# Output products of all four batches as seven for eight, and softmax totals by one transfer inside SBUF

## The chip, the cores and the metric

The kernel runs on one core of a Trainium2 chip. The core has a matmul engine (TensorE, PE in the profile), a vector engine (VectorE, DVE), an activation engine (ScalarE, ACT), a general engine (GpSimd, POOL) and a sync engine (SyncE, SP), which in this kernel issues every DMA. Each engine works through its own instructions in order and waits on semaphores. The on-chip memories are SBUF (128 partitions) and PSUM, where matmuls put their sums. The metric is the device time of one execution in microseconds (us); a run of the kernel is compared with others by the median.

## The reference

Everything is float32: 4 batches (B), 1024 tokens (N), width 1024 (DIM), 16 heads of 64.

```python
scale, shift = split(cond @ W_emb + b_emb)              # per batch
xn  = rms_norm(x, g_norm) * (1 + scale) + shift
q, k, v = split_heads(xn @ W_qkv)                       # (1024 x 1024) @ (1024 x 3072) per batch
q, k = rms_norm(q, g_q), rms_norm(k, g_k)
o   = softmax(q @ k.T / 8) @ v                          # per batch and head
x   = x + o + o @ W_out                                 # (1024 x 1024) @ (1024 x 1024) per batch
x   = x + causal_conv(x, taps = cond) + conv_bias       # 4 taps per channel; the taps are the 4 rows of cond
```

The part that this change is about is `x + o + o @ W_out` and the convolution behind it, and, in the softmax, the division by the sum of the exponentials.

## The kernel before

**Units.** Attention is cut into 64 units: for every batch b (4) and every pair of heads c (8), two halves of the queries (512 each). Unit p is batch p // 16, pair p // 2 % 8, half p % 2. A unit's scores are 8 key tiles of 128 x 1024 (`scores`, L683: matmul, copy to SBUF on ScalarE, running maximum on VectorE). The softmax (`softmax`, L732) takes the maximum over partitions on GpSimd, copies it to PSUM, subtracts on VectorE (`shift`), exponentiates on ScalarE and adds up on GpSimd (`weigh`). The unit's product with the values (`values`, L746) and its totals (`finish`, L760) are computed while the next unit's scores run. There is one PSUM tile for the product with the values (`ps_a`), so the next unit can begin its own only when `divide` (L799) has read the previous one.

**The totals.** `finish` sums the exponentials over the partitions with a matmul by ones: four groups of 256 totals, in partitions 0, 32, 64 and 96. `spread` (L781) copies them to SBUF, writes the four rows to DRAM in four transfers and reads them back as 128 partitions of 8. `invert` (L791) takes the reciprocal of this small tile on VectorE, writes it to DRAM and reads it back, repeated over the partitions, as `rec`. `divide` multiplies the product by `rec` into `oT` and stores it in DRAM (`scrO`). For the last pair of batch 3 both halves skip this way: their reciprocal is taken on the whole PSUM tile (L804), and `oT` stays in SBUF.

**The other work.** Between the stages of a unit a list of pieces runs on TensorE. Seven pieces a unit belong to x @ W_qkv (`Double.piece`, L638), which is done in Winograd's form of Strassen's scheme, seven block products for eight, for two head pairs at a time. In the units before unit 60 they fill most of the time; the last of them runs in unit 59.

**The output products.** With the block rows of o by token half and the block columns by half of the width, `o @ (W_out + 1)` is 8 products of 4 matmuls (128 x 128 by 128 x 512) for 4 output blocks (two halves of tokens, columns j and j + 4). A `Quad` (L897) computes these 4 blocks with 7 products, P1 to P7, in the order P1, P2, P6, P5, P3, P7, P4. Four of its operands are sums of blocks of o, written to DRAM by `OutSums` (L871), and four are sums of blocks of the weights, written by `OutWeights` (L842). Each product loads 1 MB of o (tag `ob`, two buffers) and 256 KB of weights (tag `wo`, three buffers). Partial sums u2 and u4 stay in SBUF. 70 such products, the ten quads of batches 0 and 1 and j = 0, 1 of batch 2, are laid into units 18 to 59 (`products_until`). The other 8 blocks of batch 2 and the 16 of batch 3 are `Out` blocks (L963): two products each (8 matmuls), whose o is loaded once (`gather`, L817) and held; VectorE adds the identity to the weights (`diagonal`, L987). Batch 2's 8 blocks lie in units 60 to 62. Of batch 3's, seven lie in unit 63 and nine behind it.

**A block's end.** x is transposed into PSUM (`residual`), the products are added, and the result, x1, is put into SBUF: with a ScalarE copy in `Out`, with a VectorE addition of u2 or u4 in `Quad`. ScalarE makes the last tap, VectorE the other three (`taps`, L1042), with a halo of three columns that the first half of the tokens leaves for the second. Later `store` transposes the result on TensorE, copies it on ScalarE and stores it.

**What sets the order.** The instructions of TensorE, VectorE, ScalarE and GpSimd run in the order in which the program emits them. A model clock moves with each emitted TensorE step (`tick`); steps for other engines are put off by so many microseconds of that clock (`defer`), into a gap after the maximum (`defer_gap`), or to the end of the softmax's busy time (`defer_quiet`), and `need` emits what has been put off when someone depends on it. SP's transfers are placed by the framework, as early as their buffers allow in its plan, and run in that order.

Of the kernel before, what the change touches and what calls it, by code (L numbers as in the profile page):

```python
# [15 lines left out]
P = 128  # L16
# [5 lines left out]
def kernel(  # L22
# [148 lines left out]
    rows = apool.tile([P, HN], F32, tag="xs", name="rows", bufs=2)[:NR, :P]  # L171
# [39 lines left out]
    class Norm:  # L211
# [10 lines left out]
        def squares(self, i):  # L222
            t0 = self.tiles[i] * P
            for g in range(2):
                xs = apool.tile([P, HN], F32, tag="xs", name=f"xs_{self.name}_{i}_{g}", bufs=2)
                nc.sync.dma_start(xs, x[self.b, t0 : t0 + P, g * HN : (g + 1) * HN])
                defer(5.0 + g, ("x", self.name), lambda xs=xs, g=g: self.square(xs, xs, i, g))
# [4 lines left out]
        def squares_of(self, i, halves):  # L232
            for g in range(2):
                to = apool.tile([P, HN], F32, tag="xs", name=f"xs_{self.name}_{i}_{g}", bufs=2)
                self.square(halves[g], to, i, g)
# [145 lines left out]
    class Embed:  # L381
# [22 lines left out]
        def run(self):  # L404
# [11 lines left out]
            sb = apool.tile([P, HN], F32, tag="xs", name=f"mod_sb_{half}", bufs=2)[:, :QN]  # L416
# [260 lines left out]
    class Unit:  # L677
        def __init__(self, pr, half):
            self.pr, self.half = pr, half
            self.name = f"{pr.b}_{pr.c}_{half}"  # L680
            self.sp = []

# [77 lines left out]
        def finish(self):  # L760
            b, c = self.pr.b, self.pr.c
            tot = ps_m.tile([P, HN], F32, tag="m", name=f"tot_{self.name}")
            for g in range(4):
                h, i = divmod(g, 2)
                some = slice(0, HN) if (b, c) == (B - 1, NJ - 1) else slice(i * QN, (i + 1) * QN)
# [9 lines left out]
            if (b, c) == (B - 1, NJ - 1):  # L775
                return
            key = ("tot", self.name)
            defer(0.2, key, lambda: self.spread(tot))
            defer(8.0, key, self.invert)

        def spread(self, tot):  # L781
# [3 lines left out]
            scr = dram.tile([4, QN], F32, tag=f"tot_{self.name}", name=f"scrT_{self.name}")  # L785
            for g in range(4):
                nc.sync.dma_start(scr[g : g + 1, :], sums[32 * g : 32 * g + 1, :QN])
            self.few = small.tile([P, 2 * HN // P], F32, tag="few", name=f"few_{self.name}", bufs=1)
            nc.sync.dma_start(self.few, scr.rearrange("g (p i) -> (g p) i", p=32))
# [9 lines left out]
        def divide(self):  # L799
            b, c = self.pr.b, self.pr.c  # L800
            need("tot", self.name)
            if (b, c) == (B - 1, NJ - 1):
# [3 lines left out]
            nc.vector.tensor_mul(oT, self.pav, self.rec)  # L806
            if (b, c) == (B - 1, NJ - 1):
# [9 lines left out]
    def gather(b, half):  # L817

        for kh in range(2):

            n = KH - kh if b == B - 1 else KH
            for k in range(n):
                need("oT", b, kh * KH + k, half)
            if half:
                four = apool.tile([P, 8, QN], F32, tag="r", name=f"ob_{b}_{kh}_{half}", bufs=2)
                four = four.rearrange("p i t -> p (i t)").rearrange("p (k t) -> p k t", t=HN)
            else:
                four = apool.tile([P, KH, HN], F32, tag="ob", name=f"ob_{b}_{kh}_{half}", bufs=2)
            nc.sync.dma_start(four[:, :n, :], scrO[b][half][:, kh * KH : kh * KH + n, :])
            for k in range(n):  # L830
                oTs[b, kh * KH + k, half] = four[:, k, :]
# [64 lines left out]

    class Quad:  # L897


        def __init__(self, b, j):  # L900
            self.b, self.j = b, j
            self.outs = {
# [4 lines left out]
        def load(self, name):  # L907
            b, j = self.b, self.j
            if name in self.outs:
                self.outs[name].load_x()  # L910
            o = self.o[name] = apool.tile([P, KH, HN], F32, tag="ob", name=f"o_{b}_{j}_{name}", bufs=2)
            if name in OUT_S:
                for k in range(KH):
                    need("S", b, k)
                src = scrS[b][:, OUT_S[name], :, :]
            else:
                half, kh = {"P1": (0, 0), "P2": (0, 1), "P4": (1, 1)}[name]
                for k in range(kh * KH, (kh + 1) * KH):
                    need("oT", b, k, half)
                src = scrO[b][half][:, kh * KH : (kh + 1) * KH, :]  # L920
            nc.sync.dma_start(o, src)
# [4 lines left out]

        def product(self, name):
            b, j = self.b, self.j
            out = self.outs.get(name)
            if name == "P7":  # L930
# [3 lines left out]
            if name in ("P2", "P3", "P4"):  # L934
                out.residual()
                pm = out.pm
            else:
                pm = ps_m.tile([P, 512], F32, tag="m", name=f"po_{b}_{j}_{name}")
            for k in range(KH):
                nc.tensor.matmul(  # L940
                    pm,
                    self.w[name][:, k, :],
                    self.o[name][:, k, :],
                    start=(k == 0 and name not in ("P2", "P3", "P4")),
                    stop=(k == KH - 1),
                )
            tick(3.5)
            if name == "P1":
                self.u2 = apool.tile([P, HN], F32, tag="ou2", name=f"ou2_{b}_{j}", bufs=1)
                nc.scalar.copy(self.u2, pm)  # L950
            elif name == "P5":
                self.u4 = apool.tile([P, HN], F32, tag="ou4", name=f"ou4_{b}_{j}", bufs=1)
# [10 lines left out]
    class Out:  # L963
# [12 lines left out]
        def load(self):  # L976
            self.load_x()
            j = self.j
            js = slice(j * P, (j + 1) * P)
            self.w = []  # L980
            for kh in range(2):
                w = wpool.tile([P, KH, P], F32, tag="wo", name=f"wo_{self.name}_{kh}", bufs=3)
                nc.sync.dma_start(w, w_out[kh * HN : (kh + 1) * HN, js].rearrange("(k p) d -> p k d", p=P))
                self.w.append(w)
            defer(4.5, ("wo", self.name), self.diagonal)

        def diagonal(self):  # L987
            d = self.w[self.j // KH][:, self.j % KH, :]
            nc.vector.tensor_tensor(d, d, ident, ALU.add)  # L989

# [13 lines left out]
        def product(self, kh):  # L1004
            b, j, half = self.b, self.j, self.half
            need("wo", self.name)
            need("oT", b, NJ - 1, half)
            for k in range(kh * KH, (kh + 1) * KH):
                nc.tensor.matmul(  # L1009
                    self.pm,  # L1010
                    self.w[kh][:, k % KH, :],
                    oTs[b, k, half],
                    start=False,
                    stop=(k == NJ - 1),
                )
            if kh == 0:
                return
            self.open()
            nc.scalar.copy(self.x1[:, PAD:], self.pm)
            self.last_tap(self.pm)  # L1020

        def open(self):

            if len(taken) == 2:
# [26 lines left out]
        def store(self):  # L1051
# [7 lines left out]
            ot = apool.tile([P, HT, P], F32, tag="x", name=f"ot_{self.name}", bufs=6)  # L1059
# [16 lines left out]
    DIVIDE = 18.0  # L1076
# [5 lines left out]
    LOUD = 5.0  # L1082
    AGE_REST = 5.0
    AGE_OWN = 8.5
    W_AT = 3
# [4 lines left out]
    outs, norms, chunks, weights, doubles, quads = {}, {}, {}, {}, {}, {}  # L1090
    LAST = (B - 1) * 2 * NJ
    NB = 2 * NJ
    ND = B * NJ // 2
    PB = NJ // 2
    LOADS_A = 2

    def piece(T):
# [27 lines left out]
        if n < ND:  # L1125
# [21 lines left out]

            if n in (PB - 1, PB) and i % 14 == W_AT:
                free(lambda: OutWeights((n - PB + 1) * 2 + i // 14).load())
# [19 lines left out]
    def out_next(m):  # L1169
        at = REST.index(m) + 1 if m in REST else 0  # L1170
        out_load(m + 1 if m not in REST else REST[at] if at < len(REST) else LAST)

    def out_load(m):
        if m < B * NB and m not in outs:
            b, i = divmod(m, NB)
# [229 lines left out]
```

## Time and profile before

| | |
|---|---|
| median of 3 runs | 2847.76 us (2844.87 to 2850.12) |
| profiled execution, its own time | 2850.32 us |
| its span, first to last instruction | 2848.5 us |
| TensorE busy | 2764.3 us, 97% of the span |
| VectorE, ScalarE, GpSimd busy | 2162.1, 1541.5, 1323.4 us |
| HBM | 411.85 MB read, 95.40 MB written, 178 GB/s over the span |

The profile has busy time by engine; groups of equal instructions with their count, busy time, mean duration, and the idle time just before them with what ended it; the chain of work that ended last; waits by who waited for whom; and a timeline. A float32 matmul appears as two instructions. Matmuls are pipelined, so the mean duration of one (some 592 ns for 128 x 512) is longer than the distance between two; distances are read from the timeline. Idle time of an engine matters where the engine is on the path that sets the end.

### The profile page before, as it was taken

How to read it: one execution, taken by the hardware profiler on the slowest of the kernel's cores; microseconds unless marked ns; L12 is line 12 of the kernel's file. 1: busy time of each engine (PE TensorE's matmuls, PEld its weight loads, DVE VectorE, ACT ScalarE, POOL GpSimd, SP SyncE). 2: the span in 40 equal slices, each digit the busy share in tenths (PEclk: the TensorE clock that was granted, in tenths of full speed). 3: DMA queues.
4: the chain of work that ended last, by engine and by line, in shares of the span. 5: the costliest groups of instructions: out<-in, count | busy, mean ns of one | idle time of the engine just before them, and what ended most of it. 6: DMA issues, size and time to landing. Idle time of an engine off the chain costs nothing.

```text
span 2848.5 us, 32001 instructions
## 1 busy us (share of the span) xinstructions
PE 2764.3 (97%) x10581; PEld 1315.6 (46%) x10581; DVE 2162.1 (76%) x2579; ACT 1541.5 (54%) x2221; POOL 1323.4 (46%) x534
## 2 busy tenths in 40 slices
PE   6999999999999999999999999999999999999998
PEld 3544444444444445444444445444444444444344
DVE  4578788877888777788777777788778867787863
ACT  4255666655555566655555556565455545555532
POOL 2055554455554454353555355354455445544520
PEclk9999999999999999999999999999999999999999
DMA  9854555645554556674565556665565444533334
GB/s 318 276 170 145 192 174 187 204 152 172 174 196 158 175 192 209 208 234 161 165 208 180 169 180 212 193 228 182 166 214 197 144 135 165 167 104 105 114 108 118
DMA packets 416844, 509.40 MB, mean 179 GB/s; under 512 B 40816, under 2 KB 326824, under 8 KB 406952
## 3 DMA queue, kind: packets, MB, share of 16 engines
q1 hardware_dynamic: 416680, 507.36, 54.6%
q8 instruction: 85, 1.39, 0.2%
q14 instruction: 79, 0.65, 0.1%
HBM read 411.85 MB, written 95.40 MB: 178 GB/s over the span
## 4 chain that ended last, share of the span: by engine, by line
PE 79%; DVE 11%; DMA 4%; ACT 2%; issue 2%; SPq 1%; POOL 0%; DVEq 0%; ACTq 0%; POOLq 0%
PE pqkv_P L648 31%; PE pav L751 16%; PE s L688 15%; PE po L1009 5%; PE po_P L940 5%; DVE mx L705 4%; PE po L940 4%; DVE sp L724 2%; PE qkt L506 1%; DVE qk L498 1%; DMA rec<-scrR 1%; ACT sp L696 1%; PE po L995 1%; PE tot L766 1%; DMA we<-in_L_cond_W_emb_dram 1%
## 5 line engine op out<-in xcount | busy, mean ns | idle before, releaser
L648 PE MATMUL pqkv_P<-w_P,a 128*128 128x384 f32 x3456 | 1177.5, 492 | 18.2 <-issue 6.6
L730 POOL TENSOR_TENSOR sum<-sum,sp 128x1024 f32<-128x1024 f32 x384 | 934.7, 2434 | 35.9 <-ACT sp L728 4.8
L648 PEld LDWEIGHTS pqkv_P<-w_P,a 128*128 128x128 f32 x3456 | 642.4, 191 | 482.7 <-issue 77.7
L696 ACT COPY sp<-s 128x1024 f32<-128x1024 f32 x512 | 501.2, 1017 | 500.1 <-PE s L688 500.0
L728 ACT ACTIVATE sp<-sp 128x1024 f32<-128x1024 f32 x512 | 531.9, 1055 | 221.3 <-DVE sp L724 217.6
L724 DVE TENSOR_TENSOR sp<-sp,mbp 128x1024 f32<-128x1024 f32 x512 | 603.5, 1209 | 21.4 <-ACT mbp L719 21.2
L710 POOL PARTITION_ALL_REDUCE mb<-mx x64 | 219.7, 3432 | 849.7 <-DVE mx L705 421.3
L705 DVE TENSOR_TENSOR mx<-mx,sp 128x1024 f32<-128x1024 f32 x384 | 486.3, 1266 | 133.2 <-ACT sp L696 103.6
L688 PE MATMUL s<-qT,kT 64*128 64x512 f32 x2048 | 509.0, 615 | 2.0 <-ACT sp L696 2.0
L751 PE MATMUL pav<-sp,v 128*64 128x512 f32 x2048 | 484.5, 605 | 17.4 <-DVE oT L806 17.1
L730 POOL TENSOR_TENSOR sum<-sp,sp 128x1024 f32<-128x1024 f32 x64 | 151.5, 2366 | 486.7 <-ACT sp L728 186.5
L688 PEld LDWEIGHTS s<-qT,kT 64*128 64x128 f32 x2048 | 175.6, 185 | 306.3 <-issue 137.6
L751 PEld LDWEIGHTS pav<-sp,v 128*64 128x64 f32 x2048 | 131.6, 137 | 334.5 <-issue 287.4
L1045 DVE SCALAR_TENSOR_TENSOR y<-x,cols,y 128x512 f32<-128x512 f32 x192 | 241.7, 1263 | 48.0 <-ACT y L1033 43.4
L705 DVE TENSOR_TENSOR mx<-sp,sp 128x1024 f32<-128x1024 f32 x64 | 105.2, 1644 | 138.2 <-ACT sp L696 138.2
L667 DVE TENSOR_TENSOR qk<-u,pqkv_P 128x256 f32<-128x256 f32 x256 | 105.7, 413 | 74.0 <-PE pqkv_P L648 73.2
L1009 PE MATMUL po<-ob,wo 128*128 128x512 f32 x352 | 155.4, 593 | 0.5 <-DVE wo L989 0.5
L940 PE MATMUL po_P<-o_P,wq_P 128*128 128x512 f32 x320 | 143.9, 592 | 0.8 <-DMA o_P<-scrS 0.8
L498 DVE TENSOR_TENSOR qk<-qk,ms 128x1024 f32<-128x1024 f32 x64 | 136.0, 2145 | 0.0
L719 ACT COPY mbp<-mb 128x1024 f32<-128x1024 f32 x64 | 65.1, 1017 | 105.6 <-POOL mb L710 105.3
L940 PE MATMUL po<-o_P,wq_P 128*128 128x512 f32 x240 | 108.0, 592 | 0.0
L485 ACT ACTIVATE sq<-qk 128x512 f32<-128x512 f32 x128 | 76.8, 628 | 55.1 <-DVE qk L667 55.1
(94 smaller groups left out, 1753.0 us busy)
## 6 DMA issues: line engine op xcount, KB each, us to landing
a<-scrA SPq DMA_DIRECT2D x212, 512.0 KB
w_P<-scrB SPq DMA_DIRECT2D x64, 768.0 KB
o_P<-scrS SPq DMA_DIRECT2D x40, 1024.0 KB
w_P<-in_L_cond_W_qkv_dram SPq DMA_DIRECT2D x192, 192.0 KB
o_P<-scrO SPq DMA_DIRECT2D x30, 1024.0 KB
scrA<-r SPq DMA_DIRECT2D x28, 896.0 KB
wq_P<-scrW SPq DMA_DIRECT2D x70, 256.0 KB
xc<-in_x_dram SPq DMA_DIRECT2D x64, 256.0 KB
```

What stands on the lines that cost most here:

```text
L648: nc.tensor.matmul(pm, (chunk.r(place) if a is None else a[:, k, :])[:, t % 2 * P : (t % 2 + 1) * P], w[:, k, :], start=(k == 0), stop=(k ...
L688: nc.tensor.matmul(ps[:, h, :], pr.kT[kt // HT][h * D : (h + 1) * D, kt % HT * P : (kt % HT + 1) * P], pr.qT[self.half][h * D : (h + 1) * ...
L696: nc.scalar.copy(sp, ps)
L705: nc.vector.tensor_max(self.mx, self.mx if kt > 1 else self.sp[0], self.sp[kt])
L710: nc.gpsimd.partition_all_reduce(self.mb.rearrange("p h q -> p (h q)"), self.mx.rearrange("p h q -> p (h q)"), P, bass_isa.ReduceOp.max,)
L724: nc.vector.tensor_sub(self.sp[kt], self.sp[kt], self.mb)
L728: nc.scalar.activation(sp, sp, AF.Exp)
L730: nc.gpsimd.tensor_tensor(self.sum, self.sum if kt > 1 else self.sp[0], sp, ALU.add)
L751: nc.tensor.matmul(self.pav[h * D : (h + 1) * D, :], self.pr.v[kt // HT][:, kt % HT, h * D : (h + 1) * D], self.sp[kt][:, h, :], start=(kt ...
L940: nc.tensor.matmul(pm, self.w[name][:, k, :], self.o[name][:, k, :], start=(k == 0 and name not in ("P2", "P3", "P4")), stop=(k == KH - 1),)
L1009: nc.tensor.matmul(self.pm, self.w[kh][:, k % KH, :], oTs[b, k, half], start=False, stop=(k == NJ - 1),)
L1045: nc.vector.scalar_tensor_tensor(self.y, self.x1[:, k : k + HN], cols[:, r : r + 1], self.y, ALU.mult, ALU.add)
```

## The change

All output products are now quads: 16 quads of 7 products, 112 in all.

- **Batch 0.** Its four P1 products need only the first half of the tokens and of the width of o. They are computed in units 14 to 17 (`ahead`), put into DRAM (`scrU`) and read back into u2 when the quad's turn comes. The weights' sums (`OutWeights`) are started in doubles 2 and 3 instead of 3 and 4, that is from unit 5 instead of 8.
- **Batches 0 and 1, and j = 0, 1 of batch 2:** the remaining 24 products of batch 0 in units 18 to 33; batch 1's 28 and the first 11 of batch 2 in units 34 to 59.
- **Batch 2, j = 2, 3:** 14 products, taken in pairs that share one load of o, in units 60 to 62, behind the last three products of j = 1 and ahead of batch 3's four P1. The second of the two quads has u2 and u4 in a buffer of tag `a`.
- **Batch 3.** A class `Last` holds the quarters of o in SBUF, loaded from DRAM apart from the last pair, which never leaves SBUF. VectorE makes the four sums there, in place or in two free weight buffers. P1 (units 60 to 62) and P7 (unit 63) are computed early and read back; P2 for j = 0, 1 is in unit 63; all the rest follows the last unit, quad by quad: two P2, then P6, P5, P3, P7 (an addition only), P4 for each j.
- **Totals.** `spread` moves the totals with a single transfer from SBUF (partitions 0, 32, 64, 96) to SBUF (128 partitions of 8). `invert` is put off by 4.5 instead of 8.0, and `divide` by 16 instead of 18. Only the last unit takes the reciprocal of the whole tile; before, the last two did.
- **Smaller.** The squares' and the embedding's scratch tiles move from tag `xs` to tag `xg`. A second-half block first emits the taps of its first half. Batch 3's output tiles use tag `qk`. `Out.load`, `diagonal` and `Out.product` are gone.

```diff
@@ finish, spread, divide
-            defer(8.0, key, self.invert)
+            defer(4.5, key, self.invert)
...
-            scr = dram.tile([4, QN], F32, tag=f"tot_{self.name}", name=f"scrT_{self.name}")
-            for g in range(4):
-                nc.sync.dma_start(scr[g : g + 1, :], sums[32 * g : 32 * g + 1, :QN])
             self.few = small.tile([P, 2 * HN // P], F32, tag="few", name=f"few_{self.name}", bufs=1)
-            nc.sync.dma_start(self.few, scr.rearrange("g (p i) -> (g p) i", p=32))
+            nc.sync.dma_start(self.few, sums[0:P:32, :QN].rearrange("g (p i) -> g p i", p=32))
...
-            if (b, c) == (B - 1, NJ - 1):
+            if self.final:
                 self.rec = apool.tile([P, HN], F32, tag="rec", name=f"rec_{self.name}", bufs=1)
                 nc.vector.reciprocal(self.rec, self.tot)
@@ class Last
+        def differences(self):
+            ws = [wpool.tile([P, KH, W3], F32, tag="w", name=f"S3_{self.b}_{i}", bufs=3) for i in range(2)]
+            ws = [w.rearrange("p k c -> p (k c)").rearrange("p (k t) -> p k t", t=HN) for w in ws]
+            self.s3 = [ws[k // 3][:, k % 3, :] for k in range(KH)]
+            for k in range(KH):
+                nc.vector.tensor_tensor(self.s3[k], self.o[0, 0][k], self.o[1, 0][k], ALU.subtract)
...
+        def sum(self, i, k):
+            o11, o12, o21, o22 = (self.part(h, kh, k) for h in range(2) for kh in range(2))
+            dst, p0, p1, op = (
+                (o21, o21, o22, ALU.add),
+                (o11, o21, o11, ALU.subtract),
+                (self.s3[k], o12, o11, ALU.subtract),
+            )[i]
+            nc.vector.tensor_tensor(dst, p0, p1, op)
@@ class Quad
+        def ahead(self, name):
+            b, j = self.b, self.j
+            pm = ps_m.tile([P, 512], F32, tag="m", name=f"pe_{b}_{j}_{name}")
+            self.multiply(pm, name, True)
+            tick(3.5)
+            t = apool.tile([P, HN], F32, tag="ue", name=f"ue_{b}_{j}_{name}", bufs=2)
+            nc.scalar.copy(t, pm)
+            nc.sync.dma_start(scrU[b, name][:, j, :], t)
@@ Out.open, the order
+            if self.half:
+                need("y", f"{self.b}_{self.j}_0")
...
-    DIVIDE = 18.0
+    DIVIDE = 16.0
-    W_AT = 3
+    W_AT = ((PB - 2, 10), (PB - 2, 24), (PB - 1, 10), (PB - 1, 24))
...
+    b2 = [(B - 2, j, name, False) for j in (0, 1) for name in OUT]
+    pair = [(B - 2, j, name, False) for name in OUT for j in (2, 3)]
+    plan(range(NB - 2, NB + 2), [(0, j, "P1", True) for j in range(KH)])
+    plan(range(NB + 2, 2 * NB + 2), [e for j in range(KH) for e in late_steps(0, j)])
+    plan(range(2 * NB + 2, B * NB - 4), [e for j in range(KH) for e in late_steps(1, j)] + b2[:-3])
+    plan(range(B * NB - 4, B * NB - 1), b2[-3:] + pair + [(B - 1, j, "P1", True) for j in range(KH)])
+    own = [(B - 1, j, "P7", True) for j in range(KH)]
+    own += [(B - 1, j, "P2", False) for j in (0, 1)]
+    plan([B * NB - 1], own)
+    end = [(B - 1, j, "P2", False) for j in (2, 3)]
+    end += [e for j in range(KH) for e in late_steps(B - 1, j) if e[2] != "P2"]
+    plan([B * NB], end)
...
-        if p == B * NB - 1:
-            gather(B - 1, 0)
-            gather(B - 1, 1)
-            stretches = [[], [], [], between(p) + own]
...
-            defer(2.7 if p > B * NB - 2 else DIVIDE, ("oT", last.pr.b, last.pr.c, last.half), last.divide)
+            defer(DIVIDE, ("oT", last.pr.b, last.pr.c, last.half), last.divide)
...
     last.divide()
+    held.sums(range(3), (KH - 1,))
+    run([piece for pieces in out_steps(B * NB) for piece in pieces])
     store()
```

## The prediction

> **What bounds the kernel now.** I read the page first: busy shares and the chain that ended last.
>
> ```profile
> PE 2764.3 (97%) x10581; PEld 1315.6 (46%) x10581; DVE 2162.1 (76%) x2579; ACT 1541.5 (54%) x2221; POOL 1323.4 (46%) x534
> PE 79%; DVE 11%; DMA 4%; ACT 2%; issue 2%; SPq 1%; POOL 0%; DVEq 0%; ACTq 0%; POOLq 0%
> ```
>
> TensorE is busy 97% and carries 79% of the chain. An average over stages hides where the other 3% is, so I cut the span at the first scores of units 0, 14, 18, 60 and 63 (columns: window, length, then busy time and instructions of PE, PEld, DVE, ACT, POOL, clock, DMA share, GB/s).
>
> ```profile
> 0.00:130.12 130.12, 107.86 (x470) 61.79 (x470) 62.47 (x139) 38.57 (x91) 17.55 (x22) 0.96 0.90 306
> 130.12:660.28 530.16, 501.14 (x1945) 235.86 (x1944) 430.64 (x516) 320.78 (x449) 279.98 (x110) 0.99 0.55 181
> 660.28:810.93 150.65, 142.20 (x546) 65.66 (x544) 119.05 (x142) 81.13 (x100) 83.33 (x33) 0.99 0.49 164
> 810.93:2571.10 1760.17, 1753.38 (x6714) 835.98 (x6712) 1375.95 (x1608) 983.63 (x1393) 857.12 (x339) 1.00 0.55 181
> 2571.10:2690.43 119.33, 113.12 (x427) 47.61 (x425) 95.32 (x90) 69.53 (x98) 54.24 (x22) 0.99 0.38 116
> 2690.43:2848.50 158.07, 146.58 (x490) 68.69 (x488) 78.71 (x85) 47.90 (x91) 31.16 (x12) 0.99 0.35 103
> ```
>
> Idle TensorE per stage is length minus PE busy: 22.3 before unit 0, 29.0 in units 0-13, 8.5 in 14-17, 6.8 in 18-59, 6.2 in 60-62, 11.5 from 63 on. Units 0-17 hold no output products, and there the largest wait is this (total, times, longest; units 0-17):
>
> ```profile
> PE pav L751 <- DVE oT L806: 12.1, 9, 2.1
> PE pqkv_P L648 <- issue: 6.6, 4, 2.6
> PE pqkv_P L648 <- DVE u L660: 4.0, 4, 1.5
> ```
>
> There is one accumulator for attention times values. The next unit's values wait until the previous unit was divided, and the division waits for the totals' way through DRAM. The timeline of unit 1 shows it, and one line of unit 20 shows that there the reciprocal waits for the read:
>
> ```profile
> 210.68 0.64 PE L766 MATMUL tot<-sum,ones 128*32 128x256 f32 x8
> 213.80 1.11 SPq L787 DMA_DIRECT2D scrT<-tots  x4
> 215.78 0.34 SPq L789 DMA_DIRECT2D few<-scrT  x1
> 222.88 0.20 DVE L792 RECIPROCAL few<-few 128x8 f32<-128x8 f32 x1
> 234.01 0.69 DVE L806 TENSOR_TENSOR oT<-pav,rec 128x512 f32<-128x512 f32 x1 [0.95 <-DMA rec<-scrR]
> ...
> 952.93 0.20 DVE L792 RECIPROCAL few<-few 128x8 f32<-128x8 f32 x1 [1.31 <-DMA few<-scrT]
> ```
>
> The end is where the products are dense (one output block; then three taps with GpSimd busy, and with it idle):
>
> ```profile
> 2809.87 6.17 PE L1009 MATMUL po<-ob,wo 128*128 128x512 f32 x14
> 2815.88 1.02 PE L1009 MATMUL po<-oT,wo 128*128 128x512 f32 x2
> 2816.74 0.60 PE L1056 MATMUL otp<-ident,y 128*128 128x128 f32 x4
> ...
> 2734.80 7.30 DVE L1045 SCALAR_TENSOR_TENSOR y<-x,cols,y 128x512 f32<-128x512 f32 x3
> ...
> 2810.49 2.33 DVE L1045 SCALAR_TENSOR_TENSOR y<-x,cols,y 128x512 f32<-128x512 f32 x3 [1.49 <-ACT y L1033]
> ```
>
> Sixteen matmul instructions take 2809.87 to 2816.74, 6.87 us, 0.43 us each with no gap. A product (4 matmuls, 8 instructions) is 3.44 us, a group of 4 transposes 0.44.
>
> **The change, part by part.** *Products.* Before: 70 products in units 18-59 (560 instructions), then 24 blocks of two: 16 in units 60-62, 32 from 63 on; 118. After: 4 in units 14-17, 24 in 18-33, 39 in 34-59, 21 in 60-62, 6 in 63, 18 behind it; 112. Six fewer are 6 x 3.44 = 20.6 us of TensorE. Where they move decides the rest.
>
> [...]
>
> *Units 0-13: -9.* The five small transfers of the totals become one. In unit 20 (whose reciprocal waits for the read) the path is: first write issued 946.22, read issued 949.00, reciprocal 952.93. An SBUF-to-SBUF transfer is not in the trace; the nearest row is that read, 3.93 us from issue to use. With it the reciprocal could run 2.8 us earlier. Bounds: zero (as slow as today's two steps, 6.7) to 6.7 (instant); I take 2.8. The reciprocal is also placed at 4.5 instead of 8.0 us and the division at 16 instead of 18, so the division leaves 2 us earlier. Nine waits of at most 2.1, 12.1 in all, 10.6 of them in units 0-13; I take 9 back (ends 0 and 10.6). Waiting at 4.5 holds VectorE's next shifts, but those wait for the maximum until 7.6 us or later behind the scores' end. SP loses four writes and the wait between write and read each unit, a release for what is queued behind it. The weights' sums move three units earlier, 0.7 us subtractions on VectorE (430.64 of 530.16 busy), at nothing: if that cover were gone, four blocks at 3.4 us, 14 us. Their transfers share two buffers with batch 0's weight blocks, needed two units later. Squares in another buffer: nothing, same depth.
>
> *Units 14-17: +6.* Four products are 13.8 us on 142.2 busy, 156; with 1 us of idle left 157, against 150.65. So 7.5 of the 13.8 falls into today's 8.5 us of idle. The copy out is 0.57 on ScalarE (81 of 151 busy).
>
> *Units 18-59: -26.* Seven products fewer (24.1) and three blocks fewer with 0.88 of transposes each (2.6) are 26.7. Batch 0's reloads of 256 KB wait on SP for the quad's last addition; loads behind them have products of 11 us in hand; I charge 0.7 (ends 0 and 4 x 5, the longest such SP wait). VectorE has 1376 of 1760.
>
> *Units 60-62: +20.* Five more products (17.2) and three more blocks (2.6) on 113.1 busy: 133. Then stalls. VectorE had 95.3; it loses 8 diagonals (4.5) and gains three blocks of 0.68 + 3 x 1.26 (13.4), eight additions instead of ScalarE copies (5.4), some ten additions of 0.68 (7), ten sums of 0.76 (7.6): 124 of 133. In unit 62 six taps ahead of the maxima already put the maximum 7.1 us behind the scores where 3.3 is usual, and the sums at 36. I charge 4 for that (ends 0 and 12, 4 per unit) and 2 for loads: the two quads share 1 MB loads, which at the trace's best slice (318 GB/s) take 3.3 us under two products of 6.9. With 6 of idle: 139, against 119.3. The 5.07 us wait for the division before unit 63's values goes, as 7 products lie in front of it.
>
> *Unit 63 and the end: -16.* Scores 13.3. Before, 14 products (48 us) covered the softmax; after, 6 and some transposes, 22.5, then 7.1 of values: ready after 29.6. Usually the sums end 31 to 33.5 us behind the scores, with blocks between 36 to 38. I take 37: a new wait of 7.4. Then totals 1.1; 18 products, 14 groups of transposes in and 14 out, 74.2 (before: 9 blocks, 71). The final division (3.35 + 0.69) and the sums behind it (2.3) lie under two P2 products (6.9) that don't need them. In the tail taps take 2.33, so VectorE has some 55 for 74. But P3, P7 and P4 of a quad end together: addition 0.7, taps by 3.95, P7's additions by 5.5, its taps by 8.0, P4's addition 8.7 us behind P3's product; three PSUM buffers then hold up the second product behind it by 1 us a quad: 4 (ends 0 and 12). The last time this is in the open: 12.2 from the last product's end, where it is 8.5 now. Sum 142.4 against 158.1.
>
> *Sum:* -9 + 6.3 - 26 + 19.7 - 15.7 = -24.7. The profiled execution took 2850.32 (span 2848.5 and 1.8 around it), giving 2825.6; it lay 2.6 over the median of the runs, so I predict 2823 against 2847.76.
>
> **The rivals.** *VectorE decides the end.* For it: 124 of 133 us, taps of 7.30 us for three, the backlog in unit 62. Against: in units 18-59 VectorE is busy up to 38 of 43 us and TensorE shows no idle time. Both upper ends, 8 more in 60-62 and 4 to 8 more behind: 2835 to 2840.
>
> *The loads decide it.* Seven 1 MB loads in 60-62 in a row with weights and blocks; if each is open for 3.3, 23 us: 2846, no change. Against: one such wait (0.8 us) in the whole trace.
>
> *The idle time closes.* Nothing new in 60-62 (-6), no wait in unit 63 beyond 2 (-5), all 10.6 and 8.5 taken: 2808 to 2810.
>
> *Slower: the direct transfer is late.* VectorE waits in order for it in 62 units. First shifts run 9.6 to 11.5 us behind the totals, and the sums end 2.4 to 5 us before TensorE needs them; so nothing is lost until the transfer lands about 14 us behind the totals. Beyond it each microsecond costs 62; at 14.5 the gain is gone, at 15 the time is 2854. Against: it would need 11 us and more, where the read took 3.93. [...]
>
> **How the numbers follow.** Forecast (2815 to 2831) 0.50; VectorE (to 2840) 0.20; closed idle (2806 to 2815) 0.14; loads 0.07, half of it within 0.2%; late transfer or a stalled queue of this size 0.09. A measurement tells 0.2%, 5.7 us, from no change. Faster 0.87, same 0.04, slower 0.09. The range 2808 to 2840 leaves some 0.2 outside.
>
> **What would show it.** Units 18-59 near 1734 us with TensorE gapless; units 1-7 near 36 instead of 37.5 and the wait for the division gone; the reciprocal 6 to 8 us behind the totals (9 to 11.5 now); units 60-62 near 139; a wait of some 7 us before the last totals; 12 us behind the last product. It is wrong if units 18-59 show new idle (queue), or if 60-62 exceed 150 (VectorE or loads).

## The result, and the profile after

The changed kernel takes 2934.97 us (median of 4 runs, 2929.66 to 2940.97), the kernel before 2846.32 on the same chip: a ratio of 1.0311, 95% interval 1.0286 to 1.0336. It is 3.1% slower; 2823 had been forecast.

The page of the changed kernel, busy time and chain:

```profile
PE 2768.6 (95%) x10533; PEld 1317.1 (45%) x10533; DVE 2223.4 (76%) x2619; ACT 1536.9 (52%) x2208; POOL 1330.2 (45%) x534
PE 79%; DVE 10%; DMA 4%; ACT 3%; issue 2%; SPq 1%; POOLq 0%; DVEq 0%; ACTq 0%
```

Busy time and chain hardly differ from before. TensorE runs 48 instructions fewer and is nevertheless busy 4.3 us longer. The stages say more. The windows of the changed kernel, cut at the first scores of units 0, 14, 18, 60 and 63 as in the prediction:

```profile
0.00:128.47 128.47, 107.24 (x470) 61.96 (x470) 62.49 (x139) 38.58 (x91) 17.56 (x22) 0.96 0.90 305
128.47:666.43 537.96, 499.25 (x1946) 234.80 (x1945) 443.16 (x526) 321.03 (x449) 279.56 (x109) 0.99 0.57 188
666.43:819.93 153.50, 153.03 (x579) 71.22 (x577) 116.56 (x132) 82.65 (x104) 83.88 (x33) 1.00 0.49 157
819.93:2552.04 1732.11, 1724.51 (x6642) 822.39 (x6641) 1387.46 (x1598) 977.82 (x1380) 860.81 (x338) 1.00 0.55 179
2552.04:2755.86 203.82, 149.96 (x490) 63.76 (x488) 117.15 (x113) 73.91 (x106) 67.13 (x26) 0.89 0.38 121
2755.86:2927.90 172.04, 134.64 (x418) 63.01 (x416) 96.55 (x111) 42.92 (x78) 21.26 (x8) 0.87 0.35 102
```

| stage | before, us | forecast | after | difference |
|---|---|---|---|---|
| units 0-13 | 530.16 | 521 | 537.96 | +7.8 |
| units 14-17 | 150.65 | 157 | 153.50 | +2.9 |
| units 18-59 | 1760.17 | 1734 | 1732.11 | -28.1 |
| units 60-62 | 119.33 | 139 | 203.82 | +84.5 |
| 63 and the end | 158.07 | 142.4 | 172.04 | +14.0 |

Two things are new in the last two windows: TensorE is idle for 53.9 and 37.4 us (length less busy), and the granted clock, 0.99 before, is 0.89 and 0.87. The waits of TensorE in the changed kernel (total, times, longest) name the first:

```profile
PE po L1077 <- DMA xc<-in_x_dram: 59.1, 15, 6.8
PE otp L1122 <- DVE y L1111: 20.0, 5, 5.4
PE xtp L312 <- DVE v L667: 9.8, 2, 6.7
...
PE pav L752 <- DVE oT L804: 0.3, 1, 0.3
```

Fifteen blocks wait for their x, 59.1 us in all. The wait for the division, 12.1 us in units 0 to 17 before, is gone as forecast (last line), and yet units 0 to 13 got longer.

The timeline of TensorE at the beginning of unit 60 shows what such a wait is, and what it leaves behind:

```profile
2564.51 3.60 PE L1017 MATMUL po<-o_P,wq_P 128*128 128x512 f32 x8
2574.96 1.09 PE L1077 MATMUL po<-ident,xc 128*128 128x128 f32 x4 [6.85 <-DMA xc<-in_x_dram]
2575.84 5.67 PE L1017 MATMUL po_P<-o_P,wq_P 128*128 128x512 f32 x8
2587.36 1.09 PE L1077 MATMUL po<-ident,xc 128*128 128x128 f32 x4 [5.86 <-DMA xc<-in_x_dram]
```

And SyncE's queue over the same stretch, in two pieces:

```profile
2567.24 0.32 SPq L792 DMA_DIRECT2D scrR<-few  x1
2568.14 0.32 SPq L994 DMA_DIRECT2D o_P<-scrO  x1
2568.63 1.10 SPq L795 DMA_DIRECT2D rec<-scrR  x2
2569.78 0.58 SPq L1069 DMA_DIRECT2D xc<-in_x_dram  x1
```

```profile
2581.53 0.33 SPq L994 DMA_DIRECT2D o_P<-scrO  x1
2581.91 0.44 SPq L1069 DMA_DIRECT2D xc<-in_x_dram  x1
```

SyncE issues in the order of its queue. In front of a block's x stands the load of o (1 MB, two buffers of tag `ob`) or of the product's weights (three of tag `wo`), and that load cannot start before a product that still runs has given its buffer back. The first product ends at 2568.11, o is issued at 2568.14 and x at 2569.78; the second ends at 2581.51, o is issued at 2581.53 and x at 2581.91. TensorE has nothing but that block's transposes next. From the issue of x to these transposes it is 5.2 and 5.5 us here, with the megabyte of o issued shortly ahead; in the waits without such a load in the 2.2 us ahead it is 3.2 to 4.5. So x pays twice, for its place in the queue and, it seems, for the bytes in front of it. Over the first wait the DMA engines are busy for 0.85 of the time and move 264 GB/s (last two columns):

```profile
2568.00:2574.80 6.80, 0.11 (x1) 0.00 (x0) 3.73 (x3) 1.94 (x4) 3.40 (x1) 0.88 0.85 264
```

From unit 60 on SyncE waits 109.9 us at weights' loads and 46.8 us at loads of o for products to end. The kernel before had waits of this kind too (123.5 us at `wo` loads), but its `out_next` asked for the next block's x before them, with two products in hand.

The second thing is the clock. A product's row is 3.60 us long where nothing disturbs it; the one behind the wait took 5.67, and four transposes took 0.88 instead of 0.44 from their start to the next start. A window over the end of these transposes and the first 2.8 us of that product:

```profile
2575.20:2578.60 3.40, 3.40 (x8) 1.85 (x8) 2.45 (x4) 0.00 (x0) 0.00 (x0) 0.50 0.00 0
```

TensorE is busy throughout at a granted clock of 0.50. From unit 60 on the same was to be seen once in the kernel before, behind its longest wait there, where 16 instructions that take 3.65 us elsewhere took 5.17:

```profile
2685.33 5.17 PE L751 MATMUL pav<-sp,v 128*64 128x512 f32 x16 [5.07 <-DVE oT L806]
```

From unit 60 on TensorE has 17 waits of 3.2 us or more, and slow work follows all but two of them (one of 3.84 us and the last one, 3.21 us); the shortest that it follows is 3.27 us long. With each of these 15 goes a stretch at a granted clock of 0.50, 3.4 to 7.0 us long in slices of 0.2 us, which begins in the wait or within 1 us behind its end.

### The profile page after: what moved, and what is told of

It reads as the page before. It is cut to its first block, busy times and chain, and to the rows that moved or that the text cites. A ratio compares the mean times of both kernels' runs of the same rounds, so it can differ in the third digit from the quotient of the medians.

```text
span 2927.9 us, 31741 instructions
## 1 busy us (share of the span) xinstructions
PE 2768.6 (95%) x10533; PEld 1317.1 (45%) x10533; DVE 2223.4 (76%) x2619; ACT 1536.9 (52%) x2208; POOL 1330.2 (45%) x534
## 3 DMA queue, kind: packets, MB, share of 16 engines
HBM read 415.53 MB, written 98.30 MB: 175 GB/s over the span
## 4 chain that ended last, share of the span: by engine, by line
PE 79%; DVE 10%; DMA 4%; ACT 3%; issue 2%; SPq 1%; POOLq 0%; DVEq 0%; ACTq 0%
PE pqkv_P L648 33%; PE pav L752 15%; PE s L689 15%; PE po_P L1017 6%; PE po L1017 5%; DVE mx L706 3%; DMA xc<-in_x_dram 2%; DVE sp L725 2%; PE qkt L506 1%; PE pe_P L1017 1%; DVE r L326 1%; PE po L1077 1%; PE tot L767 1%; DVE y L1111 1%; DMA we<-in_L_cond_W_emb_dram 1%
## 5 line engine op out<-in xcount | busy, mean ns | idle before, releaser
L689 PEld LDWEIGHTS s<-qT,kT 64*128 64x128 f32 x2048 | 175.4, 185 | 306.7 <-ACT sp L697 142.4
L1111 DVE SCALAR_TENSOR_TENSOR y<-x,cols,y 128x512 f32<-128x512 f32 x192 | 285.3, 1487 | 12.1 <-ACT y L1099 7.6
L1017 PE MATMUL po_P<-o_P,wq_P 128*128 128x512 f32 x352 | 163.2, 609 | 1.4 <-DVE v L667 1.4
L1099 ACT ACTIVATE y<-x,cols,tap_self 128x512 f32<-128x512 f32 x64 | 52.1, 814 | 206.0 <-DVE x L1053 204.0
L1017 PE MATMUL po<-o_P,wq_P 128*128 128x512 f32 x288 | 135.7, 616 | 0.0
L1077 PE MATMUL po<-ident,xc 128*128 128x128 f32 x256 | 45.1, 306 | 65.0 <-DMA xc<-in_x_dram 59.1
```

The source lines that it names most:

```text
L689: nc.tensor.matmul(ps[:, h, :], pr.kT[kt // HT][h * D : (h + 1) * D, kt % HT * P : (kt % HT + 1) * P], pr.qT[self.half][h * D : (h + 1) * ...
L1017: nc.tensor.matmul(pm, self.w[name][:, k, :], self.operand(name, k), start=start and k == 0, stop=k == KH - 1)
L1111: nc.vector.scalar_tensor_tensor(self.y, self.x1[:, k : k + HN], cols[:, r : r + 1], self.y, ALU.mult, ALU.add)
```

## The experiments

Two theories for units 60 and on. *Queue:* x is asked for behind loads that wait for a product, each wait costs itself and then half-clock time, and VectorE is not the limit. *VectorE:* it has too much to do there, and whatever wait is removed, TensorE waits for the taps or the softmax instead. For units 0 to 13: the earlier weights' sums, or the totals' new place on VectorE. Each ratio is to the kernel before on the same chip.

**x asked for ahead.** The changed kernel; from unit 60 on the x of the next two steps is asked for ahead of the current product.

```diff
+    def x_ahead(i):
+        for n in range(i + 1, min(i + 1 + AHEAD_X, len(STEPS))):    # AHEAD_X = 2
...
+            if out and not early and out.xc is None:
+                out.load_x()
...
             quad = quads[b, j]
+            if i >= PLAN[B * NB - 4][0]:
+                x_ahead(i)
```

> The changed kernel, but from unit 60 on a block's x is asked for two steps ahead and before the product of the step, so that its tile is taken ahead of the previous block's y; the same bytes. Theory Q (x is asked for one product of 3.4 us ahead while its landing takes 3 to 7 us, and each such wait also halves TensorE's clock for 3 to 7 us): TensorE's waits for x fall from 59.1 us to under 12, units 60-62 from 204 to about 160, the part from unit 63 on from 172 to about 150, the time from 2935 to 2850-2875. Rival L (the transfers themselves decide: 1 MB loads, reloads, blocks in one queue): the waits stay or move to the loads of o and weights, and the time stays 2915-2940. Rival V (VectorE decides the end): the waits move to its taps (20 us now), units 60-62 stay over 185 and the time over 2900.

Measured 2859.76 us, ratio 1.0039 (1.0025 to 1.0054): some 75 us back. Units 60 to 62 take 163.2 us and the rest 140.6. The waits of TensorE:

```profile
PE otp L1123 <- DVE y L1112: 24.5, 6, 7.0
...
PE pav L752 <- ACT sp L729: 7.2, 2, 6.5
```

The wait for x is gone from the list, and TensorE's waits for loads of o come to 1.2 us, with the same 415.53 MB read from HBM in both kernels: the order was the cause, and not the amount. The run cannot tell the earlier issue of x from its no longer being behind the megabyte of o. The wait for the taps ahead of a block's output transposes (`otp` for y) is left, 24.5 us, 19.2 of them in units 60 to 62. The wait for the last unit's softmax stands where 7.4 us had been forecast.

**Matmuls in place of the idle time.** The changed kernel with 28 transposes of the identity, whose results are overwritten, ahead of the transposes of x in 13 of the blocks that waited. This is work added, to keep the clock up.

```diff
+            if (self.b, self.j, self.half) in WAITED:
+                for i in range(28):
+                    nc.tensor.transpose(self.pm[:, i % HT * P : (i % HT + 1) * P], ident, ident)
```

> The changed kernel with 28 transposes of the identity (3.1 us) put ahead of the transposes of x in the 13 blocks that waited 3.2 to 6.9 us; their result is overwritten, nothing else moves. If the products behind a wait are slow because the idle time drops TensorE's clock: they take 3.4 to 3.6 us again instead of 4.1 to 5.6, the mean clock in units 60 and later rises from 0.88 to over 0.93, and the time falls by 8 to 22 us although TensorE does 40 us more of work. If they are slow for another reason (operands still arriving, memory traffic): they stay slow and the time is the same or up to 10 us longer.

Measured 2917.3 us, ratio 1.0236 (1.0217 to 1.0255): faster by 0.75 points with more work to do. Its windows from unit 60 and from unit 63 on:

```profile
2550.12:2750.63 200.51, 167.36 (x687) 84.06 (x685) 116.96 (x113) 73.96 (x106) 67.03 (x26) 0.92 0.39 123
2750.63:2914.70 164.07, 144.69 (x586) 77.27 (x584) 96.03 (x111) 42.94 (x78) 21.31 (x8) 0.94 0.37 107
```

TensorE's busy time there is 312.1 us; 41.9 of it are the added transposes (their group in the table of lines), so the kernel's own work took 270.2, where it took 284.6 without them. The 14.4 us are the clock's. The cure is partial: of the 13 products behind the added transposes seven have their full pace, where one had it, and the others still take up to 6.02 us, and the clock rises from 0.89 and 0.87 to 0.92 and 0.94.

**The output transposes later.** *x asked for ahead*, with one number changed: how long after a block's last product its transposes for the output are placed, in units 60 to 62.

```diff
-    AGE_REST = 5.0
+    AGE_REST = 16.0
```

> e1_x_ahead (2859.8) with one number changed: in units 60 to 62 a block's output transposes are placed 16 us behind its last product instead of 5. If TensorE stands there only because the transposes, in order in its queue, are asked for before VectorE has done the taps (24.5 us of waits on y, and the half clock behind them), most of it goes: units 60 to 62 from 163 to 140 to 148, the time 2837 to 2845. If VectorE is the bound of these units, the wait only moves to the next thing VectorE owes (the probabilities' shift, a PSUM buffer): units 60 to 62 stay at 158 to 165 and the time at 2853 to 2861.

Measured 2833.91 us, ratio 0.9953 (0.9937 to 0.9968): faster than the kernel before. The windows of units 60 to 62 and of the rest:

```profile
2550.49:2688.32 137.83, 131.65 (x482) 56.24 (x480) 119.61 (x111) 72.43 (x104) 65.10 (x25) 1.00 0.52 164
2688.32:2830.70 142.38, 124.17 (x426) 57.83 (x424) 100.20 (x114) 44.24 (x80) 24.04 (x10) 0.93 0.46 134
```

With both waits nearly gone (0.5 us for x, 5.3 for the taps, all behind unit 62) these stages take 137.8 and 142.4 us, where the prediction had 139 and 142.4. VectorE is not the limit: it does the same work in 138 us that it had done in 204, and TensorE is idle for 6.2. The output transposes had stood in TensorE's order ahead of products that were ready, before VectorE could have done the taps. Against the changed kernel this is 95.7 us in the two stages: 66.9 less idle time and 28.8 less busy time for the same products, at a granted clock of 1.00 and 0.93 instead of 0.89 and 0.87.

**The totals alone,** in the kernel before: one transfer in SBUF, the reciprocal at 4.5, the division at 16.

```diff
-            defer(8.0, key, self.invert)
+            defer(4.5, key, self.invert)
...
-            nc.sync.dma_start(self.few, scr.rearrange("g (p i) -> (g p) i", p=32))
+            nc.sync.dma_start(self.few, sums[0:P:32, :QN].rearrange("g (p i) -> g p i", p=32))
...
-    DIVIDE = 18.0
+    DIVIDE = 16.0
```

> The kernel before with the totals' part alone: one transfer inside SBUF, the reciprocal put off by 4.5 instead of 8.0, the division by 16 instead of 18. The prediction's step says -9 in units 0-13, with the wait of attention times values for the division gone. Theory now: the wait goes (12.1 us to about 0.5) but most of the time is lost again one step later, at PSUM buffers that VectorE or ScalarE empties late, so units 0-5 take about as long and the whole is 0 to 6 us faster: 2840-2846. If the step was right: 2835-2839.

Measured 2849.47 us, ratio 0.9997 (0.9987 to 1.0007): nothing. The wait for the division is gone from the list, and units 0 to 13 take 535.5 us in the profile instead of 530.2. Other waits have grown: for VectorE's `u` 5.3 us (4.0 before), without a recorded releaser at x @ W_qkv 9.3 (6.6).

**The weights' sums alone,** in the kernel before, at the change's earlier places.

```diff
-    W_AT = 3
+    W_AT = ((2, 10), (2, 24), (3, 10), (3, 24))
```

> The kernel before with the weights' sums started in doubles 2 and 3 instead of 3 and 4, nothing else. The prediction took this as free, 14 us if not. Theory: VectorE's first step of them stands in its order where the load has not landed (the buffer is still the weight blocks'), it holds the shifts of unit 8, and units 6-11 take 6 to 11 us more: time 2851-2857. If it is free: 2844-2848, and then the 8 us that units 0-13 lost in the changed kernel come from the totals' part or the shared scratch tiles.

Measured 2859.34 us, ratio 1.0032 (1.0019 to 1.0045): 9 us lost. Unit 8 takes 48.8 us instead of 42.3, units 7 and 9 3.3 and 3.5 more. The timeline of VectorE in unit 8 of the changed kernel, which takes 47.4:

```profile
439.05 6.16 DVE L565 TENSOR_TENSOR b<-b 128x384 f32<-128x384 f32 x8
445.13 2.35 DVE L498 TENSOR_TENSOR qk<-qk,ms 128x1024 f32<-128x1024 f32 x2
449.27 0.29 DVE L899 TENSOR_TENSOR W<-W,ident 128x128 f32<-128x128 f32 x1 [1.79 <-issue]
450.46 0.29 DVE L899 TENSOR_TENSOR W<-W,ident 128x128 f32<-128x128 f32 x1 [0.90 <-DMA W<-in_L_cond_W_out_dram]
```

And SyncE's queue there:

```profile
439.63 5.33 SPq L566 DMA_DIRECT2D scrB<-b  x7
445.14 0.83 SPq L892 DMA_DIRECT2D W<-in_L_cond_W_out_dram  x2
```

VectorE works in order and stands at the weights' diagonal (L899), because their load (L892) came at 445.14, behind the writes of a block of the other weights out of the buffer. Ahead of that it has eight of the other weights' sums in a row (6.16 us), where the kernel before has four (3.90). TensorE's wait for `v` there is 6.7 us, and 1.6 in the kernel before. The run with the weights' sums alone has the same picture: eight sums in 6.15 us, waits of 1.73 and 0.93 at the diagonal, and 7.1 us for `v`.

**The weights' sums at their old places,** with *x asked for ahead*; the four early products two each in units 16 and 17.

```diff
-    W_AT = ((PB - 2, 10), (PB - 2, 24), (PB - 1, 10), (PB - 1, 24))
+    W_AT = ((PB - 1, 3), (PB - 1, 17), (PB, 3), (PB, 17))
-    plan(range(NB - 2, NB + 2), [(0, j, "P1", True) for j in range(KH)])
+    plan(range(NB, NB + 2), [(0, j, "P1", True) for j in range(KH)])
```

> x asked for two steps ahead, as in e1_x_ahead (2859.8), and the weights' four sums back at their old places (units 8 to 14); batch 0's four early products then stand two each in units 16 and 17. If the earlier weights' sums are what cost units 0 to 13 their time (the same move alone cost the old kernel 9 us), unit 8 goes back from 47 to about 42 us, units 0 to 13 to 530 to 535, and the time to 2847 to 2853. If the loss in units 0 to 13 comes from the totals' earlier wait on VectorE instead, the time stays at 2857 to 2862.

Measured 2869.21 us, ratio 1.0072 (1.0054 to 1.009): 9 us slower than *x asked for ahead* where 7 to 13 faster had been expected. The first half of the expectation held: units 0 to 13 take 530.4 us instead of 541.2. But units 14 to 17 take 175.9 us instead of 153.2, 21 of it in unit 16, which has two early products now instead of one and the longest wait:

```profile
769.63 6.20 PE L1017 MATMUL pe_P<-o_P,wq_P 128*128 128x512 f32 x8 [15.00 <-DMA o_P<-scrO]
```

The first early product's o takes one of the same two `ob` buffers, which now hold the weights' sums and the sums of o; its load was issued at 762.3, behind the write of the weights' sums. The next two runs have this edit too, and its 15 us. The first has both edits, this one and `AGE_REST = 16.0`:

> Both: x ahead, weights' sums at their old places, output transposes later. If the two losses are independent the gains add: 2826 to 2836, faster than the kernel before by 0.5 to 0.8%, which is where the count of products had put it. If VectorE binds units 60 to 62: about 2847 to 2852, no change.

Measured 2848.72 us, ratio 0.9997 (0.9988 to 1.0006). The later transposes take 20 us off here, and 26 without the moved sums.

The second has the third P2 product in unit 63 on top:

```diff
-    own += [(B - 1, j, "P2", False) for j in (0, 1)]
+    own += [(B - 1, j, "P2", False) for j in (0, 1, 2)]
...
-    end = [(B - 1, j, "P2", False) for j in (2, 3)]
+    end = [(B - 1, j, "P2", False) for j in (3,)]
```

> As e7_both, with the third of batch 3's four P2 products moved from behind the last unit into it, so that 3.9 us more of TensorE's work lie ahead of the last values. If the last unit's wait for the softmax (7.2 us in e1_x_ahead) is exposed for lack of work alone, it shrinks by about 4 and the time by 2 to 4 against e7_both. If VectorE then ends later, since another block's taps stand ahead of the sums in its order, the wait stays and the time is that of e7_both or 1 to 3 longer.

Measured 2845.21 us, ratio 0.9985 (0.9976 to 0.9993). The wait for the softmax shrinks from 6.5 to 3.5 us, and the medians differ by 3.5; the intervals overlap a little.

**The weights' sums one a unit,** in units 8 to 11, with *x asked for ahead*, the later transposes and the third P2.

```diff
-    W_AT = ((PB - 2, 10), (PB - 2, 24), (PB - 1, 10), (PB - 1, 24))
+    W_AT = ((PB - 1, 3), (PB - 1, 10), (PB - 1, 17), (PB - 1, 24))
```

> e6_store_later (2833.9) with two edits: the third P2 product in the last unit, which was worth 3.5 us between e7_both and e8_third_p2, and the weights' four sums at one a unit in units 8 to 11, so that the first comes no earlier than in the kernel before, and all are done two units ahead of batch 0's early products, which stay in units 14 to 17. If the weights' sums cost units 0 to 13 their 8 to 10 us because the second one's load met the weight blocks of batch 0 in unit 8, these units go back to 530 to 535 and the time to 2819 to 2826. If sums closer together cost VectorE the same (four blocks of a combine each in four units), units 0 to 13 stay at 537 to 542 and the time is 2828 to 2833. If the early products have to wait for their loads as in e5_weights_late, 2840 or more.

Measured 2841.28 us, ratio 0.9973 (0.9962 to 0.9985). This is slower than the 2819 to 2833 of the first two cases, and the third does not explain it, since the early products do not wait. Unit 8 is cured (43.3 us), and unit 12 takes 48.8 instead of 36. VectorE there, and the wait of SyncE between 600 and 625 us:

```profile
607.60 2.86 DVE L933 TENSOR_TENSOR S<-S 128x512 f32<-128x512 f32 x4
619.41 0.29 DVE L899 TENSOR_TENSOR W<-W,ident 128x128 f32<-128x128 f32 x1 [8.95 <-DMA W<-in_L_cond_W_out_dram]
```

```profile
SPq L892 <- DMA scrS<-S: 3.9, 1, 3.9
```

The same figure as in unit 8 with another owner of the buffer: the weights' load waits until the sums of o are written out (L934), and VectorE stands in order behind it.

The same with the totals' old way through DRAM, the reverse of the edit under *the totals alone*:

> e9_weights_between with the totals' way of the kernel before (through DRAM in five transfers, the reciprocal placed at 8 us and the division at 16 to 18): all else alike. The prediction had the new way at 9 us faster; alone on the old kernel it gave nothing (ratio 0.9997). If it is worth nothing here either, the two are within 3 us of each other; if the wait for the division was what its gain went into, this one is 6 to 10 us slower.

Measured 2844.28 us, ratio 0.9981 (0.9972 to 0.999). Units 0 to 13 take 551.3 us against 548.4. The wait for the division is back with 8.3 us, and the time differs by less than the intervals: the new way is worth at most a few microseconds.

With the fourth load in unit 12 instead of 11, and the totals' new way:

```diff
-    W_AT = ((PB - 1, 3), (PB - 1, 10), (PB - 1, 17), (PB - 1, 24))
+    W_AT = ((PB - 1, 3), (PB - 1, 10), (PB - 1, 17), (PB, 3))
```

> e9_weights_between (2841.3) with only the fourth of the weights' four loads moved, from unit 11 to unit 12. There VectorE stood 9 us in order at the weights' diagonal in unit 12, since its load waited on SP for the write of the sums of o (scrS) out of the buffer that it was to take; TensorE stood 11.0 us. If that buffer is the cause, as it was unit 8's in the changed kernel, units 0 to 13 go from 548 to 530 to 537 and the time to 2824 to 2832. If VectorE has simply too much to do there, the wait moves to unit 13 or 14 and the time stays at 2838 to 2843.

Measured 2841.46 us, ratio 0.9984 (0.9975 to 0.9993). Units 0 to 13 take 535.8 us, as expected of the buffer; but the time stays, since the first early product then waits 13.6 us in unit 14:

```profile
699.13 1.19 PE L1017 MATMUL pe_P<-o_P,wq_P 128*128 128x512 f32 x1 [13.63 <-issue]
```

The expectation that a wait in unit 14 would mean too much work for VectorE was badly put: it is again a load that comes late, and units 12 and 13 lost nothing. That this wait is for the `ob` buffers too was not separated by a run.

**The best of these,** with the weights' sums left where the change put them: x ahead, `AGE_REST = 16.0` and the third P2.

> e6_store_later (2833.9) with the third P2 product in the last unit and the weights' sums left where the change put them, since every other place for them met the two shared 1 MB buffers in unit 12, 14 or 16. Unit 63's wait for the softmax goes from 7.3 to 3 to 4 us, the time to 2829 to 2833, 0.6 to 0.7% below the kernel before. If the block's taps ahead of the sums on VectorE take the gain back, 2834.

Measured 2833.81 us, ratio 0.9943 (0.993 to 0.9955). It beats both kernels; what the third P2 adds to *the output transposes later* cannot be told from nothing.

## Why the prediction was wrong, step by step

**Units 60 to 62 (the failed step: "I charge 4 for that ... and 2 for loads").** The count of work was right: with the two waits taken away these units take 137.8 us, where 139 had been forecast. The 2 us for loads looked at bandwidth, 1 MB loads under two products; the loads that were late are x, 256 KB, and late for their place in SyncE's order: issued behind a load whose buffer a running product holds, and where that is o, moved beside its megabyte. They cost 59.1 us of waits from unit 60 on, and 1.2 us of waits for o were left once x was asked for earlier. The diff showed this: x moved from a call made one block ahead into the load of the next step, made behind the current product. The prediction went through the queue for units 0 to 13 and 18 to 59 but not here. The rival "the loads decide it" had the right queue, with 23 us and the wrong loads, and its "against" (one such wait of 0.8 us before) was read off a kernel that asked for x earlier.

**The clock (a term left out).** A wait was charged at its length. Here the waits cost some 40% on top: 28.8 us of busy time beside 66.9 idle in the two last stages. The line of 5.17 us in the trace before would have given the price.

**Four for VectorE.** The wait for taps was 20.0 us in all, 24.5 once x was ahead. It was neither the softmax backlog that the 4 us stood for nor the rival's VectorE as a bound, but five microseconds of model time between a block's product and its transposes, where blocks now follow each other. A number in the plan took it away.

**Unit 63 and the end (142.4 forecast).** 172.0 in the changed kernel, of which x and the clock are the excess: with x ahead 140.6, with the later transposes 142.4. The new wait for the softmax was 7.2 and 7.3 in these two runs for 7.4. Behind the last product the changed kernel takes 8.6 us and the one with the later transposes 11.8, for 12.2. That the stage agrees to a tenth is luck: the terms that the prediction lists add up to 141.8, not 142.4.

**Units 18 to 59 (-26).** -28.1, with 7.6 us of idle time in 1732: right. The seven products fewer of these units are time: TensorE's busy time fell by 28.9 us, from 1753.38 to 1724.51, and the stage by 28.1.

**Units 14 to 17 (+6.3).** +2.9: TensorE's busy time rose by 10.8 us instead of the 13.8 of four products, and idle time of 0.5 us is left where 1 had been assumed.

**Units 0 to 13 (-9).** +7.8. Two steps failed. "The weights' sums move three units earlier ... at nothing" cost 9 us: the prediction named the two shared buffers, but looked at who needs them two units later and not at who still held them; VectorE then stands in order. And "I take 9 back" took a wait that is off the limit for time: the wait did go, 12.1 to 0.3 us, and neither the old kernel (ratio 0.9997) nor the mended one (2.9 us in these units) got faster by as much. The bound was misread too: of the 12.1 us 8.4 lie in units 0 to 13, and not 10.6, since a wait of 2.1 us at 694.27 belongs to unit 14, which begins at 660.28; so 9 was more than the wait held there. The sign for it failed as well: units 1 to 7 took 36.8 us on average before, not 37.5, and 37.3 after. Which work takes the gain in units 0 to 13 is not settled; it is spread over waits of 3 us and less for VectorE and in x @ W_qkv. The transfer itself was quicker than the row taken for it: the reciprocal runs as early as 2.37 us behind its issue, against 3.93, and in none of the 63 units did VectorE stand idle for it. So the slower rival, a late transfer, did not happen.

**The chances.** 0.09 for slower, with queue stalls folded into the rival about the totals. No case for units 60 and on priced a load behind a buffer that a running product holds.

## What to carry to other kernels

When a change regroups steps, write out for each load what stands ahead of it in its queue and which buffer that one waits for; a small load behind a big one whose buffer is in use starts only when the work that it should hide behind is over (here x was issued 1.67 and 0.40 us behind the end of that product). Price a wait on TensorE at its length and the half-clock work behind it where it is as long as those that had such work behind them in the changed kernel, 3.27 us and more. A wait that vanishes is not time gained until the stage is shorter.

## What the runs showed of the hardware

- In the changed kernel from unit 60 on, the granted clock was 0.50 for 3.4 to 7.0 us at 15 of the 17 waits of 3.2 to 6.9 us, from within the wait or from within 1 us behind its end, and the matmuls behind these waits took up to twice as long (four transposes 0.88 us for 0.44, a product 5.67 for 3.60). Added matmuls in the idle time made the kernel faster by 0.75 points, though they are 41.9 us of work.
- A transfer of four rows of 1 KB from SBUF to SBUF was done within 2.37 us of its issue (2564.64, with the reciprocal at 2567.01, which had not waited), where the read of the same totals from DRAM had taken 3.93 to the reciprocal that waited for it.
- Where TensorE waited for x (256 KB) from unit 60 on in the changed kernel, it had it 3.2 to 4.5 us after its issue, and after 5.2 to 5.7 where a load of 1 MB had been issued in the 2.2 us ahead.
